# Attention's matmuls as 64x64 tiles, values in two PSUM banks, and VectorE adding the second bank in the drain

## The chip, the cores and the metric

The kernel runs on one core of one Trainium2 chip. Such a core has TensorE (PE in the profile, with its weight loads as PEld), VectorE (DVE), ScalarE (ACT), GpSimd (POOL) and SyncE (SP, which here only issues DMAs). TensorE reads SBUF and writes PSUM; VectorE and ScalarE read both; in this kernel GpSimd and the DMAs touch SBUF and DRAM alone. The metric is the device time of one execution in microseconds. Three timed executions of the kernel before took 3159.02, 3157.11 and 3157.24 us, so the median is 3157.24.

## The reference

The input x is 8 images of 512 channels and 32x32 places, in float32. Two blocks follow each other.

Layer 0 is an attention block of 8 heads with 64 channels each: group norm (32 groups), a 512 to 1536 projection, softmax attention over the 1024 places per head, a 512 to 512 projection, a second group norm, and the residual. Layer 1 is a single-head attention over all 512 channels with normalised weights and a root-mean-square norm of the projections.

```python
hn  = group_norm(x, gn1_scale, gn1_bias)
q, k, v = split(einsum('bchw,oc->bohw', hn, w_qkv) + b_qkv)      # per head: 64 channels x 1024 places
wgt = softmax(einsum('bct,bcs->bts', q * 64**-0.25, k * 64**-0.25))
a   = einsum('bts,bcs->bct', wgt, v)
x   = x + group_norm(einsum('bchw,oc->bohw', a, w_proj) + b_proj, gn2_scale, gn2_bias)
# layer 1
q, k, v = split(rms_normed(einsum('oc,bcn->bon', w_qkv1, x)))
x   = (x + w_out1 @ (softmax(q.T @ k * 512**-0.5) applied to v)) / sqrt(2)
```

## The kernel before

**Order.** Every engine is wrapped in `InOrder` (L24), so each engine executes its instructions in the order in which the code writes them. What stands earlier in an engine's queue and waits holds up all that stands behind it, SP's DMAs too. All arithmetic is float32; the hardware runs each float32 matmul as two passes, each with its own weight load, so the profile counts two matmul records for one in the code.

**Memory.** `Slots` (L39) hands out seven SBUF tiles of 16 KB per partition, first freed, first taken. PSUM has eight banks: `ps_s` holds three tiles of two banks (`wide` and the scores), `ps_m` two tiles of one bank (`bank`).

**Attention of layer 0**, the class `Heads` (L562). The eight heads are taken as four pairs j; a pair's two heads lie on partitions 0 to 63 and 64 to 127 (`halves`). For each pair the 1024 query places are eight rows of 128, so a batch has 32 steps i = 8j + r. One `step` (L635) does, in this order: `softmax(i)` (VectorE takes each head's maximum, ScalarE takes exp from PSUM and sums it); in every second step from i = 5 on, i odd, the `values` (L610) of a group of two earlier rows; the functions in `fill`, among them in even steps one piece of the projection that makes the next pair's q and k; `scores(i + 1)`; `turn`, in which VectorE transposes the probabilities of the step before and SP sends them in four DMAs to the group's tile pT; then `scale`, in which GpSimd divides the probabilities by their sum; last the functions in `later`, among them GpSimd's adds for the projections.

Scores are matmuls over the 64 channels of a head, on 64 rows and 128 columns of the array, the two heads in turn. Values are matmuls over 128 key places with 64 output channels, on 128 rows and 64 columns, the two heads in turn, all added in one bank `po`; ScalarE moves that to `a`, with the bias.

**Projections.** `project_rows` (L398) makes q and k in batch 0, and pair 0 of each next batch. It splits the 128 input channels in two halves of 64 rows with one bank each; ScalarE moves both out and GpSimd adds them. `project_seven` (L476) serves pairs 1 to 3 of the later batches: seven products stand for the eight of q and k over both halves of the places. Product 0 uses all 128 rows and one bank, the products 1 to 3 of both halves run as pairs on 64 rows each. Each of its four pieces (product 0; pairs 1, 2, 3) is one `yield`, and so one even step. As the first piece is short, the loop over i (L1433) puts two of the eight parts of the next values beside it in the first step of pairs 1 and 2 (`values(..., 2)`); the bank stays open till the step after.

**Drain.** After the 32 steps two groups of values are left, 14 and 15. Between them lie products of the next batch's v (`project_v7`, in the profile p_v_B and p_v_T), whose sums VectorE drains from three `ps_s` tiles. The code around it, with L1505 to L1525:

```python
heads.values(STEPS // RG - 2)      # group 14
heads.turn()                       # transpose of step 31, and its four DMAs
Seven.drain()                      # VectorE's waiting drains
fetch("proj7", b)                  # SP: weights of the output projection
...                                # VectorE: sums of a; ten products of v
heads.values(STEPS // RG - 1)      # group 15
...
finish_layer0(...)                 # output projection: p_o_B first, then p_o_T
```

The last batch has no next v; `LastOut` (L665) covers its drain with shares of its output projection (pp in the profile).

**Norm of batch 1 in batch 0's steps.** From i = 14 (k = 0 at L1461) the steps of the group norm's coefficients run one per step; two of them are a small matmul on TensorE (pm, pv) with a `ps_m` bank, and VectorE follows each.

## Time and profile before

| | |
|---|---|
| median of three timed executions | 3157.24 us |
| profiled execution | 3158.3 us |
| its span | 3156.5 us |
| granted TensorE clock, mean | 0.998 |
| PE busy | 3128.6 us, 13014 matmul records |
| s (scores), 64 rows x 128 columns, 512 wide | 2048 records, 510.5 us |
| po (values), 128 rows x 64 columns, 256 wide | 4096 records, 473.4 us |
| pq (project_seven), 64 x 128 | 1008 records, 452.8 us |
| pq, 128 x 128 | 84 records, 40.9 us |
| pqk (project_rows), 64 x 128 | 640 records, 144.3 us |
| DVE busy | 2366.4 us |
| ACT busy | 1070.1 us |
| POOL busy | 1409.5 us |

A busy time is the union of an engine's records within the group. Matmuls overlap each other, and their ends are modelled, so the distance from one start to the next tells more than the length of a record. In the timeline, a row merges neighbouring instructions of one kind: start, length, engine, line, operation, output and inputs with shapes (for PE, rows*columns of the tile used), their number, and in brackets the idle time of the engine before them with what ended it. All instructions bear L34, the line of the recording helper, so the names of tiles tell them apart.

### The profile page before, as it was taken

What the parts mean: (1) busy time and instruction counts of PE and PEld (TensorE: products, weight loads), DVE (VectorE), ACT (ScalarE), POOL (GpSimd) and SP (SyncE); (2) the same over time, 40 slices, a digit from 0 to 9 for tenths busy, and PEclk for the clock granted to TensorE, in tenths of its full rate; (3) what the DMA queues carried; (4) which work ended last, traced back from release to release, by engine and by line L of the source; (5) the groups of instructions that cost most, each with busy time, mean ns of one, the idle gap of its engine ahead of it and who ended that gap; (6) DMA issues with size and microseconds to landing.
All of it is one profiled execution on the core that took longest, in us unless ns stands there. A gap on an engine that the chain in (4) does not pass through costs nothing.

```text
span 3156.5 us, 36568 instructions
## 1 busy us (share of the span) xinstructions
PE 3128.6 (99%) x13014; PEld 1613.1 (51%) x13014; DVE 2366.4 (75%) x3213; ACT 1070.1 (34%) x1844; POOL 1409.5 (45%) x1129
## 2 busy tenths in 40 slices
PE   9999999999999999999999999999999999999899
PEld 5445544456444554545545555445554455444454
DVE  5697777876788767886678876787677877778765
ACT  2453124521245212551125502354133531245311
POOL 1554236732367314771247703566235642356124
PEclk9999999999999999999999999999999999999999
DMA  6777225862168521784128832388224872158600
GB/s 207 208 203 232 77 57 158 215 203 67 57 180 230 178 55 60 206 231 153 47 79 227 225 117 51 114 219 227 91 68 119 217 230 77 30 159 213 194 7 33
DMA packets 230317, 451.56 MB, mean 143 GB/s; under 512 B 22100, under 2 KB 62840, under 8 KB 224376
## 3 DMA queue, kind: packets, MB, share of 16 engines
q1 hardware_dynamic: 230016, 449.20, 50.4%
q8 instruction: 104, 1.70, 0.2%
q14 instruction: 77, 0.63, 0.1%
q10 hardware_dynamic: 120, 0.02, 0.0%
HBM read 137.26 MB, written 29.56 MB: 53 GB/s over the span
## 4 chain that ended last, share of the span: by engine, by line
PE 88%; DMA 3%; POOL 3%; DVE 3%; SPq 1%; issue 1%; ACT 0%; DVEq 0%; ACTq 0%; POOLq 0%
PE s L34 12%; PE po L34 12%; PE p L34 7%; PE p_v_T L34 6%; PE pq L34 6%; PE p_v_B L34 5%; PE py L34 4%; PE pqk L34 4%; PE pa L34 4%; PE p_u_T L34 4%; PE pe_e L34 3%; PE pe_bc L34 3%; PE pe_a L34 3%; PE p_o_T L34 3%; PE p_u_B L34 3%; DMA pT<-pb 2%
## 5 line engine op out<-in xcount | busy, mean ns | idle before, releaser
L34 ACT ACTIVATE p<-s,nm 128x1024 f32<-128x1024 f32 x512 | 565.6, 1109 | 796.0 <-DVE nm L34 461.0
L34 POOL TENSOR_SCALAR p<-p,tt 128x1024 f32<-128x1024 f32 x512 | 566.0, 1118 | 413.5 <-DVE tt L34 405.4
L34 DVE TENSOR_REDUCE nm<-s 128x1 f32<-128x1024 f32 x512 | 602.2, 1217 | 138.1 <-PE s L34 137.0
L34 DVE STREAM_TRANSPOSE pb<-p 128x2048 f32<-128x2048 f32 x256 | 590.0, 2305 | 54.7 <-DMA pT<-pb 36.2
L34 PE MATMUL s<-qk 64*128 64x512 f32 x2048 | 510.5, 605 | 0.7 <-POOL qk L34 0.5
L34 PE MATMUL po<-pT,v 128*64 128x256 f32 x4096 | 473.4, 383 | 2.4 <-DMA pT<-pb 1.5
L34 PEld LDWEIGHTS po<-pT,v 128*64 128x64 f32 x4096 | 283.2, 137 | 228.5 <-issue 29.9
L34 PEld LDWEIGHTS s<-qk 64*128 64x128 f32 x2048 | 193.2, 186 | 242.7 <-issue 214.5
L34 PE MATMUL p<-e,v 128*128 128x512 f32 (+1 forms) x520 | 229.9, 594 | 2.5 <-DVE x L34 2.5
L34 POOL TENSOR_TENSOR x<-x,o 128x1024 f32<-128x1024 f32 x21 | 52.1, 2509 | 349.0 <-ACT o L34 349.0
L34 POOL TENSOR_TENSOR esum<-esum,e 128x512 f32<-128x512 f32 x96 | 141.6, 1499 | 148.3 <-ACT e L34 148.3
L34 POOL TENSOR_TENSOR u<-u,xy 128x512 f32<-128x512 f32 x64 | 79.2, 1268 | 278.1 <-DMA xy<-far_rinv 273.5
L34 PE MATMUL pq<-hn,qk 64*128 64x512 f32 (+1 forms) x420 | 191.8, 593 | 0.0
L34 ACT ACTIVATE e<-e,shift,rinv 128x512 f32<-128x512 f32 x96 | 75.8, 810 | 269.0 <-DVE e L34 269.0
L34 DVE TENSOR_TENSOR v<-v,p_v_T 128x256 f32<-128x256 f32 x300 | 114.3, 416 | 68.8 <-PE p_v_T L34 50.0
L34 PEld LDWEIGHTS p<-e,v 128*128 128x128 f32 x520 | 98.1, 192 | 130.5 <-issue 121.3
L34 PE MATMUL pqk<-hn,qk 64*128 64x512 f32 (+1 forms) x672 | 158.2, 590 | 0.0
L34 PE MATMUL pq<-t,qk 64*128 64x512 f32 x336 | 151.0, 589 | 0.0
L34 PE MATMUL pq<-v,qk 64*128 64x512 f32 x336 | 150.9, 589 | 0.0
L34 POOL TENSOR_TENSOR esum<-e 128x512 f32<-128x512 f32 x16 | 25.1, 1586 | 274.7 <-ACT e L34 274.7
L34 PE MATMUL py<-x,gram 128*128 128x512 f32 x320 | 141.2, 601 | 4.4 <-DVE x L34 4.4
L34 POOL TENSOR_TENSOR qk<-qk,v 128x512 f32<-128x512 f32 x96 | 127.2, 1334 | 3.2 <-ACT v L34 1.6
(240 smaller groups left out, 4737.7 us busy)
## 6 DMA issues: line engine op xcount, KB each, us to landing
pT<-pb SPq DMA_DIRECT2D x1024, 256.0 KB, 4.6
qk<-far_qk SPq DMA_DIRECT2D x21, 896.0 KB
hn<-in_x_dram SPq DMA_DIRECT2D x32, 512.0 KB, 4.8
x<-in_x_dram SPq DMA_DIRECT2D x32, 512.0 KB, 3.9
out_dram<-x SPq DMA_DIRECT2D x63, 256.0 KB, 2.8
score<-far_score SPq DMA_DIRECT2D x8, 1792.0 KB, 11.8
value<-far_value SPq DMA_DIRECT2D x8, 1792.0 KB
proj<-far_proj SPq DMA_DIRECT2D x7, 1792.0 KB
```

Of the source, the lines that this page charges most:

```text
L34: return lambda *args, **kw: self._pin(call(*args, **kw))
```

## The change

A new helper `quads` issues each product as four matmuls of 64 rows and 64 columns: for each of two row halves, both column halves. Scores, both projections and values all use 64x64 tiles.

- `values` splits its 128 key places in two halves of 64 rows, each with a bank of its own. ScalarE moves the first bank to `a`, with the bias. The second bank is copied by ScalarE into the group's pT tile, which is no longer needed, and GpSimd adds that to `a`; in the drain's two calls VectorE adds the second bank from PSUM instead. pT is given back after that.
- `values` no longer runs in parts; the two parts beside the first piece of `project_seven` are gone.
- `project_seven` has again four pieces: product 1 with product 0 for the lower half of their columns, the same for the upper half, then products 2 and 3. Product 0 is split in two row halves, whose sums GpSimd adds.
- The small norm products of batch 1 are issued in even steps: the coefficient steps run two at k = 0 and k = 2, none at k = 1 and k = 3.

```diff
--- before.py
+++ after.py
@@ -370,6 +370,12 @@
     STEPS, LAG = CI * NB, 5
     halves = (slice(0, D), slice(D, P))
 
+    def quads(outs, left, right, first=True, last=True):
+
+        for out_, l, r in zip(outs, left, right):
+            for cs in halves:
+                PE.matmul(out_[cs], l[:, cs], r, start=first, stop=last)
+
     def project_qk(b, j, hn):
 
         qk = pair.tile([P, 2, N], F32, tag="qk", name=f"qk_{b}_{j}")
@@ -411,14 +417,7 @@
                     hs = slice(th * HN, (th + 1) * HN)
                     pms = [bank(f"pqk_{b}_{j}_{t}_{th}_{r}") for r in range(2)]
                     for ci in range(CI):
-                        for r in range(2):
-                            PE.matmul(
-                                pms[r],
-                                w[halves[r], ci, :],
-                                hn[halves[r], ci, hs],
-                                start=(ci == 0),
-                                stop=(ci == CI - 1),
-                            )
+                        quads(pms, [w[rs, ci, :] for rs in halves], [hn[rs, ci, hs] for rs in halves], ci == 0, ci == CI - 1)
                     to, rest = qk[:, 0, hs], spare[:, hs]
                     if t:
 
@@ -486,30 +485,41 @@
             return lambda: PO.tensor_add(to, a, b_)
 
         def pieces():
-            pm = bank(f"pq7_{b}_{j}_0")
-            run(matmuls(pm, [(w[:, k, :], right(None, 0, k)) for k in range(2)]))
-            AC.copy(tmp[1], pm)
-            yield [], []
             qk = pair.tile([P, 2, N], F32, tag="qk", name=f"qk_{b}_{j}")
             made(qk)
             kp = qk[:, 1, :].rearrange("p (be m) -> p be m", be=4)
             q1, q2 = (qk[:, 0, th * HN : (th + 1) * HN] for th in range(2))
             k1, k2 = (kp[:, :, th * P : (th + 1) * P] for th in range(2))
-            adds = (
-                ([], []),
-                ([], []),
-                ([add(q2, q2, q1), add(k2, k2, turned(q2))], [add(k1, k1, k2), add(k2, k2, turned(tmp[1]))]),
-                ([add(q1, q1, tmp[0]), add(q2, q2, tmp[1])], [add(q2, q2, tmp[2])]),
-            )
-            for n in range(1, 4):
+            adds = {
+                2: ([add(q2, q2, q1), add(k2, k2, turned(q2))], [add(k1, k1, k2), add(k2, k2, turned(tmp[1]))]),
+                3: ([add(q1, q1, tmp[0]), add(q2, q2, tmp[1])], [add(q2, q2, tmp[2])]),
+            }
+
+            def product(pms, n, cols, to):
+                count = CI if n else 2
+                for k in range(count):
+                    quads(
+                        [pm[:, to] for pm in pms],
+                        [w[rs, max(CI * n - 2, 0) + k, :] for rs in halves],
+                        [(right(r, n, k) if n else right(None, 0, k)[rs])[:, cols] for r, rs in enumerate(halves)],
+                        k == 0,
+                        k == count - 1,
+                    )
+
+            low, high = slice(0, TG), slice(TG, HN)
+            for n, cols in enumerate((low, high)):
                 pms = [bank(f"pq7_{b}_{j}_{n}_{r}") for r in range(2)]
-                for k in range(CI):
-                    for r in range(2):
-                        PE.matmul(pms[r], w[halves[r], CI * n - 2 + k, :], right(r, n, k), start=(k == 0), stop=(k == CI - 1))
-                if n == 1:
-                    AC.activation(q1, pms[0], AF.Identity, bias=bqs[:, j : j + 1])
-                    AC.copy(k1, turned(pms[1]))
-                elif n == 2:
+                product(pms, 1, cols, low)
+                product(pms, 0, cols, high)
+                AC.activation(q1[:, cols], pms[0][:, low], AF.Identity, bias=bqs[:, j : j + 1])
+                AC.copy(tmp[1][:, cols], pms[0][:, high])
+                AC.copy(k1[:, :, n * D : (n + 1) * D], turned(pms[1][:, low]))
+                AC.copy(q2[:, cols], pms[1][:, high])
+                yield [add(tmp[1][:, cols], tmp[1][:, cols], q2[:, cols])], []
+            for n in range(2, 4):
+                pms = [bank(f"pq7_{b}_{j}_{n}_{r}") for r in range(2)]
+                product(pms, n, slice(0, HN), slice(0, HN))
+                if n == 2:
 
                     AC.copy(q2, pms[0])
                     AC.activation(k2, turned(pms[1]), AF.Identity, bias=bkq[:, j : j + 1])
@@ -553,7 +563,7 @@
         def __init__(self, b, hn, v, qk):
             self.b, self.hn, self.v, self.a = b, hn, v, None
             self.qk = {0: qk}
-            self.pT, self.ps, self.waiting, self.open = {}, None, None, None
+            self.pT, self.ps, self.waiting = {}, None, None
 
         def scores(self, i):
             j, r = divmod(i, NB)
@@ -561,14 +571,11 @@
             self.ps = [ps_s.tile([P, N], F32, tag="sc", name=f"s0_{self.b}_{i}_{hh}") for hh in range(2)]
             for c in range(2):
                 cs = slice(c * HN, (c + 1) * HN)
-                for hh in range(2):
-                    PE.matmul(
-                        self.ps[hh][:, cs],
-                        qk[halves[hh], 0, r * P : (r + 1) * P],
-                        qk[halves[hh], 1, cs],
-                        start=True,
-                        stop=True,
-                    )
+                quads(
+                    [ps[:, cs] for ps in self.ps],
+                    [qk[rs, 0, r * P : (r + 1) * P] for rs in halves],
+                    [qk[rs, 1, cs] for rs in halves],
+                )
 
         def softmax(self, i):
             p = prob.tile([P, 4, 2, N // 4], F32, tag="p", name=f"p0_{self.b}_{i}")
@@ -607,28 +614,27 @@
                 PO.tensor_scalar(p[:, :, hh, :], p[:, :, hh, :], tot[:, hh : hh + 1], 1.0, ALU.mult, ALU.mult)
             self.waiting = (i, p)
 
-        def values(self, g, most=NT):
+        def values(self, g, engine=PO):
 
             j, t0 = g // (NB // RG), g % (NB // RG) * TG
-            po, s0 = self.open or (bank(f"po0_{self.b}_{g}", TG), 0)
-            s1 = min(s0 + most, NT)
-            self.open = (po, s1) if s1 < NT else None
+            pos = [bank(f"po0_{self.b}_{g}_{r}", TG) for r in range(2)]
             if self.a is None:
                 self.a = big(f"a_{self.b}")
-            for s in range(s0, s1):
-                for hh in range(2):
-                    ch = (2 * j + hh) * D
-                    PE.matmul(
-                        po[halves[hh], :],
-                        self.v[:, s, ch : ch + D],
-                        self.pT[g][:, :, :, hh, s, :],
-                        start=(s == 0),
-                        stop=(s == NT - 1),
-                    )
-            if self.open:
-                return
-
-            AC.activation(self.a[:, j, t0 : t0 + TG], po, AF.Identity, bias=col(BV, j))
+            pT = self.pT[g]
+            for s in range(NT):
+                for po, rs in zip(pos, halves):
+                    for hh in range(2):
+                        ch = (2 * j + hh) * D
+                        PE.matmul(
+                            po[halves[hh], :], self.v[rs, s, ch : ch + D], pT[rs, :, :, hh, s, :], start=(s == 0), stop=(s == NT - 1)
+                        )
+            a, rest = self.a[:, j, t0 : t0 + TG], pT[:, 0, 0, 0].rearrange("p B j -> p (B j)")
+            AC.activation(a, pos[0], AF.Identity, bias=col(BV, j))
+            if engine is VE:
+                VE.tensor_add(a, a, pos[1])
+            else:
+                AC.copy(rest, pos[1])
+                PO.tensor_add(a, a, rest)
             slots.give(f"pT_{self.b}_{g}")
             del self.pT[g]
 
@@ -1428,9 +1434,6 @@
             early, later = [], []
             if i < CI:
                 fill, later = fills[i] + fill, laters[i]
-            if b and r == 0 and 0 < j < CI - 1:
-
-                fill.append(lambda: heads.values((i + 1 - LAG) // RG, 2))
             if r == 0:
                 if j + 1 < CI:
                     if b:
@@ -1461,9 +1464,9 @@
                 k = i - 3 * CI - 2
                 if k == 0:
                     coeffs = norm1.gn.all_steps()
-                    early += [norm1.aggregate, lambda: next(coeffs)]
-                elif 0 < k < 8:
-                    early.append(lambda: next(coeffs, None))
+                    early.append(norm1.aggregate)
+                if 0 <= k < 8 and k not in (1, 3):
+                    early += [lambda: next(coeffs, None)] * (2 if k in (0, 2) else 1)
                 if 0 <= k - 7 < CI // 2:
                     for ci in range(2):
                         later.append(lambda ci=ci: norm1.apply(2 * (k - 7) + ci, PO))
@@ -1502,7 +1505,7 @@
             last = LastOut(b, heads, o_last)
             last.first_half()
             last.sums(0, 0)
-        heads.values(STEPS // RG - 2)
+        heads.values(STEPS // RG - 2, VE)
         heads.turn()
         if more:
             Seven.drain()
@@ -1522,7 +1525,7 @@
             for ci in (2, 3):
                 load_x(b, xt, ci)
             fetch("score", b)
-        heads.values(STEPS // RG - 1)
+        heads.values(STEPS // RG - 1, VE)
         slots.give(f"v0_{b}")
         if more:
             xt = big(f"x_{b}")
```

## Prediction

> **What bounds the kernel now.** First the page's parts 1 and 4: TensorE (PE) is busy 99% of the span and is 88% of the chain that ended last, so each microsecond in which PE streams nothing is a microsecond of the kernel.
>
> ```profile
> PE 3128.6 (99%) x13014; PEld 1613.1 (51%) x13014; DVE 2366.4 (75%) x3213; ACT 1070.1 (34%) x1844; POOL 1409.5 (45%) x1129
> PE 88%; DMA 3%; POOL 3%; DVE 3%; SPq 1%; issue 1%; ACT 0%; DVEq 0%; ACTq 0%; POOLq 0%
> ```
>
> Then the timeline of two attention steps of batch 3 (start, length, engine, operation).
>
> ```profile
> 1402.89 1.99 PE L34 MATMUL s<-qk 64*128 64x512 f32 x8
> 1404.71 3.60 PE L34 MATMUL pqk<-hn,qk 64*128 64x512 f32 x16
> 1404.91 2.36 DVE L34 TENSOR_REDUCE nm<-s 128x1 f32<-128x1024 f32 x2 [0.90 <-PE s L34]
> 1406.22 1.11 ACT L34 ACTIVATE p<-s,nm 128x1024 f32<-128x1024 f32 x1 [2.74 <-DVE nm L34]
> 1407.24 0.19 ACT L34 ACTIVATION_READ_ACCUMULATOR p<-s,nm 128x1 f32 x1
> 1407.33 1.10 ACT L34 ACTIVATE p<-s,nm 128x1024 f32<-128x1024 f32 x1
> 1408.14 1.88 PE L34 MATMUL s<-qk 64*128 64x512 f32 x8
> 1408.42 0.69 ACT L34 ACTIVATE qk<-pqk,bqs 128x512 f32<-128x512 f32 x1
> 1408.99 0.59 ACT L34 COPY spare<-pqk 128x512 f32<-128x512 f32 x1
> 1409.96 3.67 PE L34 MATMUL po<-pT,v 128*64 128x256 f32 x32
> ```
>
> Each fp32 product is two PE passes. 16 pqk records take 1408.14-1404.71 = 3.43 us: eight slots of 0.429, two tiles at once. A po slot (256 columns) is 0.2156 by the single records. The two steps are 2x4 slots of s, 8 of pqk and 16 of po: 10.31 us, but they repeat after 10.67 (1402.89, and the next s at 1413.56). The other 0.35 lies only where the tile shape changes: s to po 0.10 before it and 0.05 after its first slot, po to s 0.10 and 0.105. pqk to s, one shape, costs nothing.
>
> Last, the timeline of the drain after the 32 steps of that batch.
>
> ```profile
> 1427.69 2.31 DVE L34 STREAM_TRANSPOSE pb<-p 128x2048 f32<-128x2048 f32 x1 [2.34 <-POOL p L34]
> 1427.88 3.67 PE L34 MATMUL po<-pT,v 128*64 128x256 f32 x32
> 1431.60 0.47 ACT L34 ACTIVATE a<-po,cols 128x256 f32<-128x256 f32 x1 [6.78 <-PE po L34]
> 1432.37 0.75 DVE L34 TENSOR_TENSOR v<-v,p_v_T 128x256 f32<-128x256 f32 x2 [2.37 <-ACT v L34]
> 1433.13 1.26 SPq L34 DMA_DIRECT2D proj<-far_proj  x1
> 1436.05 2.73 DVE L34 TENSOR_TENSOR v<-v,p_v_T 128x256 f32<-128x256 f32 x8
> 1436.85 3.72 PE L34 MATMUL p_v_B<-v,hn 128*128 128x256 f32 x16
> 1440.50 3.67 PE L34 MATMUL po<-pT,v 128*64 128x256 f32 x32
> ```
>
> The last transpose runs beside the values of group 14; its four DMAs and then proj go out behind it on SP. By the packets, proj lands 11.3 to 14.0 us after the transpose's end (seven batches), and p_o_B, which needs it, starts at 1444.11 with 0 to 2.5 us to spare.
>
> **The change part by part.**
>
> *Tile shapes.* The program's order has 118 changes po to s (0.205) and 110 s to po (0.147); all go: -40.4 us. The 14 short pq7 products in 128x128 between s and po, with their own changes (0.10+0.10 and 0.09+0.05), go too: -4.8. Changes between attention and the 128x128 products of other stages stay, and I price them as now.
>
> *Streaming.* Twice as many matmuls of half the columns. If four tiles run at once, the slots are as many as before: s 439, po 442, pqk 137 us. pq7 pays 0.6 us for shorter slots. No row has 64x64; the nearest are 64x128 and 128x64, where two tiles start 7 ns apart and run beside each other, their weight loads too. Bounds: 0 (four together) to +1271 us (two at a time: all the attention slots, 1271, once more). I take 0, since tiles split both by rows and by columns run together here. For issue, values need 8 records per 0.2156 slot, 27 ns each. After a stall at 191.43 us PE's sequencer passed 64 such records in 1.39 us, 22 ns each. That is enough, by little.
>
> *Short pieces.* pq7's four pieces were 1.72, 3.43, 3.43, 3.43 us, with two of eight value steps moved beside the first; now 2.59, 2.59, 3.43, 3.43 and the values whole. Take 0 at the end of s, 1404.71. The first exp is read out at 1407.43, +2.72; only then is its PSUM tile free for the second head of the next s. A 2.59 us piece ends earlier: +0.19 us with 0.06 for the semaphore. Then the banks: ACT empties the piece after the second exp, from +3.71 (1408.42), now with four operations. Act 128x256 takes 0.47 (0.38 apart), copies 0.37 (0.27 apart by the two v copies of the drain): the last ends at +5.0. Values now need both banks; PE gets there at 2.78+1.72 = 4.50 and waits till 5.06: +0.56. Queued behind that wait: values, the next s, and by it DVE and ACT. For full pieces ACT ends at +4.87 and PE comes at 5.15: no wait, 0.2 to spare. This happens at i = 3, 8, 10, 16, 18 of seven batches (at i = 0 the fifth product covers it): 35x0.75 = +26.4. Bounds: 0, if ACT were early, to 35x1.3 if every copy took the 0.59 of a 512-column one. I take the 256-column rows.
>
> *Values in two banks.* ACT gets a copy (0.37) per group and POOL an add of 128x256 (half of 1.28, 0.64), ahead of the scaling in POOL's queue. In a value step ACT ends its pair at about +4.4 and the next piece wants the banks at +5.17. POOL's add ends at +5.1; scaling then ends at +7.35, and the transpose wants it at about +7.6. Nothing added, with 0.25 to spare; if that cover is gone the add costs up to 0.4 in each of 100 steps, 40 us. pT is given back after POOL's add, some 1.5 us later than now; it is refilled for use 20 us on. The same number of pT DMAs goes out, in the same order.
>
> *The drain.* VectorE's add for group 14 stands ahead of the last transpose in DVE's queue, and waits for po 14 and ACT. po's last slot starts at 1431.17; ACT ends at 1432.07, the add (0.42 by the v adds) lets the transpose start at 1432.5 and end at 1434.8 instead of 1430.0: 4.8 us later. Behind it: four pT DMAs and proj on SP, and on DVE the drains that free the banks of p_v. The latter: T2's drain frees T1's bank 0.5 late, T3's drain frees p_v_B's 1.9 later still, so the last values start 2.4 late. The former: proj lands 4.8 later; with each batch's own slack (1.1, 2.5, 0, 0.5, 0.3, 0, 0.3) p_o_B starts 3.7, 2.3, 4.8, 4.3, 4.5, 4.8, 4.5 later, 29 in all; I take 27, since the DMA before it is out of the way by then. The two run beside each other; the later counts. Bounds: 17 (DVE's alone) to 34. In the last batch the transpose ends at 2957.96 and the last po starts at 2965.79, having waited for pT. The add moves that end to 2964.5: +6.5, and the last add is bare: +0.5. Together +34. VectorE's add for group 15 is covered by p_o_B's 3.5 us.
>
> *Norm products.* Once, in batch 0: the same two small products at other steps; VectorE waits about 1 us for each inside a step with 0.5 slack. 0, bounds -1 to +2.
>
> *Sum.* -40.4 -4.8 +0.6 +26.4 +34 = +15.8 us against the profiled execution, 3158.3 us (span 3156.5 and 1.8 around it): 3174.1. The median of the runs shown is 1.1 lower, so 3173.
>
> A rule weighed against this: the Trainium skill, "TensorE: Matmul & The Clock Gate", Part 3, says that matmuls start and end strictly in program order. The program issues both passes of a tile before the next tile, so by that rule a second pass would hold up the other three tiles, four tiles would do the work of two, and the sum would be 3158+1271 = about 4430. In this trace the first passes of the two s tiles start at 1402.888 and 1402.895, the second tile ahead of the first's second pass: tiles overtake each other here, so I go by the row.
>
> **The rivals.**
> *A, faster: the short pieces don't wait.* If ACT empties the banks before PE comes, the 26.4 go and the time is 3147. For: ACT is busy only 34%. Against: its order puts the second exp first, and that ends at +3.81 in every ordinary step. It turns to faster when the wait is under 0.1 us in place of 0.75.
> *B: the second bank's copy or POOL's add is late in ordinary value steps too.* Margins are 0.2 to 0.3 us; 0.3 us in 100 steps gives 3203.
> *C: the four tiles don't all run at once*: up to 4430 (two at a time).
> *D: PE's issue binds in the values.* The densest lasting row is 54 ns per record; were that the limit, a group would take 6.9 instead of 3.45 us: +440, 3610. Against: the 22 ns above.
> *E: the drain is hidden*, because proj comes sooner without other traffic: 17 instead of 27, 3163.
>
> **How the numbers follow.** Main 53%, E 12%, A 13%, B 12%, C 5%, D 5%. The likeliest gives 3173 (its own range 3160 to 3188). C and D, 10%, stay out above; 3146 to 3215 holds the others but for some tails of A and B. A measurement tells 0.2% (6.3 us) from no change. Faster is most of A and a little of E: 0.15; within 0.2%, parts of E, A and main: 0.09; slower the rest: 0.76.
>
> **What the profile after would show.** Right: PE matmuls of 64*64 only, in s, po, pqk and pq; a pair of steps in batch 0 of 10.3 instead of 10.67 us; PE waiting for ACT before po after each short pq piece; in the drain the transpose only after po 14, and p_o_B after a wait for proj of a microsecond or more. Wrong: po groups longer than 3.5 us (C or D), no wait before po (A), p_o_B as early as now (E), or waits before pqk in every step (B).

## The result and the profile after

The changed kernel takes 3209.19 us (median of 4 runs, 3205.75 to 3213.86), the kernel before 3157.54 (4 runs beside it, 3157.11 to 3159.02): ratio 1.0165, 95% interval 1.0152 to 1.0177. It is slower, as forecast, but by 52 us where the sum said 16. It lies inside the stated range, which reached up beyond rival B's 3203; the sum's own range ended at 3188. The profiled execution took 3213.9 us (span 3212.1), 55.6 us more of span than the one before; the accounts below are between these two spans.

Parts 1 and 4 of the page of the kernel after, busy time by engine and the chain that ended last:

```profile
PE 3129.9 (97%) x22066; PEld 1717.4 (53%) x22066; DVE 2372.1 (74%) x3229; ACT 1112.4 (35%) x2061; POOL 1517.7 (47%) x1283
PE 61%; POOL 12%; issue 8%; DMA 8%; DVE 6%; SPq 3%; ACT 2%; DVEq 0%; POOLq 0%; ACTq 0%
```

PE is busy for as long as before (3128.6), with 9052 more instructions. What grew is the time in which it waits: PE's share of the chain fell from 88 to 61%, and GpSimd's (POOL) rose from 3 to 12% though it is busy less than half the time. What PE waited for, first after, then before (total us, times, longest):

```profile
PE s L34 <- POOL qk L34: 11.8, 18, 1.1
PE p_v_B L34 <- DVE v L34: 11.7, 7, 1.7
PE pq L34 <- DVE v L34: 6.2, 7, 0.9
PE p_o_B L34 <- DMA proj<-far_proj: 5.8, 4, 1.6
```

```profile
PE s L34 <- POOL qk L34: 0.5, 2, 0.4
PE p_o_B L34 <- DMA proj<-far_proj: 0.7, 2, 0.4
```

The two rows of p_v_B and p_o_B are the drain and were forecast. The two of s and pq were not: the scores of a new unit (one q and k, eight steps) wait for GpSimd's adds to q, and the first short piece waits for VectorE's v adds. The latter comes once in each of seven batches, the former 18 times, against twice before.

The drain of batch 3 (batches are counted from 0) in the timeline after:

```profile
1456.21 3.69 PE L34 MATMUL po<-pT,v 64*64 64x256 f32 x64 [1.69 <-issue]
1459.92 0.47 ACT L34 ACTIVATE a<-po,cols 128x256 f32<-128x256 f32 x1 [7.87 <-PE po L34]
1460.43 0.42 DVE L34 TENSOR_TENSOR a<-a,po 128x256 f32<-128x256 f32 x1 [7.83 <-ACT a L34]
1460.77 2.31 DVE L34 STREAM_TRANSPOSE pb<-p 128x2048 f32<-128x2048 f32 x1
1466.51 1.70 SPq L34 DMA_DIRECT2D proj<-far_proj  x1
1467.43 3.72 PE L34 MATMUL p_v_B<-v,hn 128*128 128x256 f32 x16 [1.68 <-DVE v L34]
1471.08 3.68 PE L34 MATMUL po<-pT,v 64*64 64x256 f32 x64
1476.26 1.10 PE L34 MATMUL p_o_B<-a,proj 128*128 128x512 f32 x2 [1.49 <-DMA proj<-far_proj]
```

The transpose that ran beside po 14 before now starts 4.56 us after po 14 does; behind it come proj's DMA and, on DVE, the drains that free PE's banks. A po group of 64 records of 64x64 takes 3.68 us, as the 32 of 128x64 did (3.67): four tiles run at once.

The first step of a batch (batch 3, i = 0) after:

```profile
1276.76 0.65 PE L34 MATMUL pq<-hn,qk 64*64 64x256 f32 x4
1276.95 0.69 DVE L34 TENSOR_TENSOR v<-v,p 128x512 f32<-128x512 f32 x1
1277.56 0.68 DVE L34 TENSOR_TENSOR v<-parts,p 128x512 f32<-128x512 f32 x1
1278.29 0.43 PE L34 MATMUL pq<-t,qk 64*64 64x256 f32 x2 [0.88 <-DVE v L34]
```

The piece needs two banks, one for each row half. The first row half (pq<-hn) has its bank and runs four records. The other (pq<-t) may not start until VectorE's two adds have emptied the second bank, in which the fifth of v's seven products lies. It starts 1.53 us after the first, of which PE stands idle for 0.88.

And the short piece of i = 8 with the values behind it, batch 4:

```profile
1717.31 2.14 PE L34 MATMUL s<-qk 64*64 64x512 f32 x16
1717.36 1.11 ACT L34 ACTIVATE p<-s,nm 128x1024 f32<-128x1024 f32 x1
1718.80 0.38 ACT L34 COPY v<-pq 128x256 f32<-128x256 f32 x1
1719.06 0.68 ACT L34 COPY qk<-pq 128x256 f32<-128x256 f32 x2
1719.24 0.19 PEld L34 LDWEIGHTS po<-pT,v 64*64 64x64 f32 x4 [0.67 <-ACT v L34]
1719.79 3.00 PEld L34 LDWEIGHTS po<-pT,v 64*64 64x64 f32 x58 [0.35 <-ACT qk L34]
```

The first row half of PE is through with its scores at 1717.31 + 1.72 = 1719.03, the second, which had waited for the first exp, 0.26 later. The last copy of the piece ends at 1719.74, and the second bank's tiles start there, 0.5 us late. The wait is where the prediction put it.

Where the steps changed: us against the kernel before, from the start of the last score matmul of step i to that of step i + 1, in the one profiled run of each kernel, as a mean over batches 1 to 7. The columns are the kernel after and six of the experiments below, in their order: the last transposes first; the four pieces of before; values in one bank; the load alone in the kernel before; VectorE adding in every value step, with the last transposes first; and VectorE adding at i = 5, 13, 21 and 29, with the last transposes first and the pieces of before. Row 31 is the drain, up to the next batch's first scores, as a mean over batches 0 to 6.

```
 i   after  turn_first  old_pieces  one_bank  before+load  VectorE all  VectorE i%8=5
 0    2.35     2.35       -0.04       2.35       0.00         2.35        -0.04
 3   -0.61    -0.61        0.03      -0.61       0.00        -0.61        -0.00
 4    0.55     0.55        0.00       0.55       0.00         0.55         0.00
 6    0.54     0.17        0.02       0.01       0.01         1.09         0.95
 7    0.58     0.69        0.89       0.09       0.49        -0.43        -0.46
 8   -0.30    -0.30       -0.30      -0.30      -0.00        -0.47        -0.48
 9    1.09     1.06        0.51       0.82       0.00         1.04         0.51
10   -0.91    -0.97       -0.12      -0.73      -0.12        -0.93        -0.12
11   -0.38    -0.27       -0.24      -0.18      -0.61         0.19        -0.20
12    0.01     0.01        0.01      -0.00       0.01         0.88         0.01
13   -0.35    -0.35       -0.35      -0.04       0.00        -0.35        -0.35
15    0.53     0.66        0.57      -0.04       0.23        -0.35        -0.30
16   -0.30    -0.30       -0.30      -0.30       0.15        -0.46        -0.35
17    1.06     1.06        0.51       0.82       0.00         0.71         0.51
18   -0.84    -0.84        0.00      -0.61       0.00        -0.83         0.00
19    0.24     0.03       -0.35      -0.04       0.00         0.03        -0.35
23    0.15    -0.13       -0.06      -0.04       0.26        -0.33        -0.26
31    4.79     1.30        4.84      -0.19       0.01        -0.21        -0.21
```

An undisturbed value step (13, 21, 25, 27, 29) gains 0.28 to 0.35, what the tile shapes promised. The drain loses 4.8, the first step 2.35, and the steps ahead of a new unit, 7, 15 and 23, lose where they should gain. The span's 55.6 us are: within the steps 12.1, the seven drains 33.5, the last batch's tail 9.6, the head 0.4.

### The profile page after: what moved, and what is told of

Same layout as the page of the kernel before. It is cut to its first block, busy times and chain, and to the rows that moved or that the text cites. A ratio compares the mean times of both kernels' runs of the same rounds, so it can differ in the third digit from the quotient of the medians.

```text
span 3212.1 us, 55636 instructions
## 1 busy us (share of the span) xinstructions
PE 3129.9 (97%) x22066; PEld 1717.4 (53%) x22066; DVE 2372.1 (74%) x3229; ACT 1112.4 (35%) x2061; POOL 1517.7 (47%) x1283
## 4 chain that ended last, share of the span: by engine, by line
PE 61%; POOL 12%; issue 8%; DMA 8%; DVE 6%; SPq 3%; ACT 2%; DVEq 0%; POOLq 0%; ACTq 0%
POOL p L34 6%; PE po L34 6%; PE s L34 5%; PE p_v_T L34 5%; DMA pT<-pb 5%; PE py L34 4%; PE p_v_B L34 4%; DVE pb L34 4%; PE p_u_T L34 3%; PE pe_a L34 3%; PE pe_e L34 3%; PE pe_bc L34 3%; PE p_o_T L34 3%; POOL qk L34 3%; PE pa L34 3%
## 5 line engine op out<-in xcount | busy, mean ns | idle before, releaser
L34 PE MATMUL s<-qk 64*64 64x512 f32 x4096 | 555.8, 593 | 13.8 <-POOL qk L34 11.8
L34 PE MATMUL po<-pT,v 64*64 64x256 f32 x8192 | 506.0, 379 | 6.0 <-DMA pT<-pb 3.1
L34 PEld LDWEIGHTS po<-pT,v 64*64 64x64 f32 x8192 | 361.6, 133 | 159.2 <-issue 22.0
L34 PEld LDWEIGHTS s<-qk 64*64 64x64 f32 x4096 | 206.3, 133 | 229.9 <-issue 152.2
L34 PE MATMUL pq<-hn,qk 64*64 64x256 f32 (+1 forms) x1680 | 202.3, 420 | 0.0
L34 PE MATMUL pqk<-hn,qk 64*64 64x512 f32 (+1 forms) x1312 | 162.9, 590 | 0.0
L34 PE MATMUL pq<-t,qk 64*64 64x256 f32 (+1 forms) x1008 | 156.2, 449 | 6.2 <-DVE v L34 6.2
L34 PE MATMUL pq<-v,qk 64*64 64x512 f32 x672 | 151.7, 590 | 0.0
L34 PEld LDWEIGHTS pq<-hn,qk 64*64 64x64 f32 x1680 | 100.0, 133 | 58.5 <-issue 30.3
```

Of the source, the lines that this page charges most:

```text
L34: return lambda *args, **kw: self._pin(call(*args, **kw))
```

## The experiments

**The last transposes ahead of the values of group 14.**

```
-        heads.values(STEPS // RG - 2, VE)
         heads.turn()
+        heads.values(STEPS // RG - 2, VE)
```

> The changed kernel with one move: in the drain the last transposes are issued ahead of the values of group 14, so that VectorE's add for group 14 no longer stands before them. Theory (the drain is the largest of the losses): in the trace after, the last slot of po 14 is followed by p_o_B after 16.68 to 18.24 us in seven batches, against 12.93 to 13.38 before, 29.0 us in all, and the last batch's tail is 9.6 longer. Both should go back but for the adds themselves: p_o_B 12.9 to 13.6 us after po 14, and a time of 3209 - 29 - 6 = about 3174 (3169 to 3180). Rival (the drain waits for proj or pT for another reason than the add, such as GpSimd's later queue or the give-back of pT): p_o_B stays 16 to 18 us after po 14 and the time stays within 8 us of 3209.

Measured: 3179.84 us, ratio to the kernel before 1.0066 (1.0049 to 1.0083). The drain of batch 4, from the timeline of this kernel:

```profile
1821.02 3.69 PE L34 MATMUL po<-pT,v 64*64 64x256 f32 x64
1821.31 2.31 DVE L34 STREAM_TRANSPOSE pb<-p 128x2048 f32<-128x2048 f32 x1 [2.67 <-POOL p L34]
1825.24 0.42 DVE L34 TENSOR_TENSOR a<-a,po 128x256 f32<-128x256 f32 x1 [1.62 <-ACT a L34]
1837.31 1.13 PE L34 MATMUL p_o_B<-a,proj 128*128 128x512 f32 x2
```

The transpose lies beside po 14 again and p_o_B waits for nothing. From po 14's last slot to p_o_B it is 12.99 to 13.17 us in six of seven batches (14.97 in the last), against 16.68 to 18.24. The order on DVE is what cost the drain: 29 of the 35 us expected came back. In the profiled run two drains stay long, those of batches 3 and 6, by 4.1 and 3.8 us; in batch 3 po 14 stopped for 1.4 us in its middle. Why those two, no run tells. The last batch's tail also keeps 5.0 of its 9.6 us. There VectorE's add for group 14 still stands ahead of its sums of pp, and PE waits 0.56 and 1.50 us for these before the last values.

**The four pieces of before.**

```
+            pm = bank(f"pq7_{b}_{j}_0")
+            run(matmuls(pm, [(w[:, k, :], right(None, 0, k)) for k in range(2)]))
+            AC.copy(tmp[1], pm)
+            yield [], []
-            for n, cols in enumerate((low, high)):
-                ...
-            for n in range(2, 4):
+            for n in range(1, 4):
                 pms = [bank(f"pq7_{b}_{j}_{n}_{r}") for r in range(2)]
                 product(pms, n, slice(0, HN), slice(0, HN))
```

> The changed kernel with the four pq7 pieces of before (product 0 alone, 128x128 in one bank, then three pairs of 512 columns), so that no piece has two short halves in two banks and GpSimd gets two adds fewer for each unit; the values stay whole, in two banks. Theory: the steps that lose at short pieces come back: i=0 (+2.35 us in seven batches, 16.5 in all), the 0.56 us waits for the banks at i=4, 9, 11, 17, 19 (about 20 us in all), against which the short products' own tile changes return (+4.8), and part of the late q adds of GpSimd at i=7, 15, 23 (16 in all): 3209 - 16 - 20 + 5 - 5 = about 3173 (3163 to 3190). Rival (the second bank's copy and add are what is late, whatever the piece): the steps behind a first piece still wait for ACT's copies, since PE comes to the values sooner behind a 1.72 us piece than behind a 2.59 us one; then the time is 3200 to 3215.

Measured: 3197.31 us, 1.0120 (1.0102 to 1.0139): 12 us of the 36 expected. The table says why. The loss of i=0 is gone, 2.39 us in each of seven batches, and the wait at 19. But i=3 and 4 add up to what they did (0.03, and -0.06 with the new pieces), and i=8 to 10 and 16 to 18 to a little more (0.09 and 0.21 for -0.12 and -0.08): behind a piece of 1.72 us PE comes sooner to the next scores and to the values, and waits there (in batch 4 at i=8 the weight loads of the second head's scores wait 0.57 us for ACT's exp, those of the values 0.43 us for ACT's copy). That part is the rival's. And i=7 and 15 lose as much as ever, with two GpSimd adds fewer for each unit.

**GpSimd's add of the second bank at the end of its step.**

```
-                PO.tensor_add(a, a, rest)
-            slots.give(f"pT_{self.b}_{g}")
+                def ended():
+                    PO.tensor_add(a, a, rest)
+                    slots.give(f"pT_{self.b}_{g}")
+                self.ending = ended
...
             for f in later:
                 f()
+            if self.ending:
+                self.ending()
```

> The changed kernel with GpSimd's add of the values' second bank (and the give-back of pT behind it) moved to the end of its step, behind the scaling and the adds of the pieces. Theory (GpSimd's queue, with this add in front, is what makes s wait for q at i=7, 15, 23, where it loses 16.2 us against the ordinary 0.35 gain): the waits of s for GpSimd's add of qk fall from 11.8 us to under 4 and the time to 3195 to 3201. Rival (these waits come from the longer chain of the pieces, whose own adds are last in the queue either way; or what GpSimd saves early is paid by a later add of the values): 3206 to 3212.

Measured: 3219.55 us, 1.0191 (1.0174 to 1.0207), 10 us slower than the kernel after: a miss. The waits of s for GpSimd rose to 13.8 us. Both expectations had taken the add to be in the way of its own step; the second half of the rival was nearest. The timeline of the kernel after shows what happens at the end of a unit (batch 4, i=13 to 15):

```profile
1738.66 2.14 PE L34 MATMUL s<-qk 64*64 64x512 f32 x16
1740.95 2.21 POOL L34 TENSOR_SCALAR p<-p,tt 128x1024 f32<-128x1024 f32 x2 [2.57 <-DVE tt L34]
1743.13 2.91 POOL L34 TENSOR_TENSOR qk<-qk 128x512 f32<-128x512 f32 x2
1746.00 0.72 POOL L34 TENSOR_TENSOR a<-a,pT 128x256 f32<-128x256 f32 x1
1746.71 2.21 POOL L34 TENSOR_SCALAR p<-p,tt 128x1024 f32<-128x1024 f32 x2
1748.88 1.28 POOL L34 TENSOR_TENSOR qk<-qk 128x512 f32<-128x512 f32 x1
1748.98 2.14 PE L34 MATMUL s<-qk 64*64 64x512 f32 x16
1750.24 1.55 POOL L34 TENSOR_TENSOR qk<-qk,v 128x512 f32<-128x512 f32 x1
1751.76 2.23 POOL L34 TENSOR_SCALAR p<-p,tt 128x1024 f32<-128x1024 f32 x2
1753.93 2.53 POOL L34 TENSOR_TENSOR qk<-qk,v 128x512 f32<-128x512 f32 x2
1755.29 1.95 PE L34 MATMUL s<-qk 64*64 64x512 f32 x16 [0.71 <-POOL qk L34]
1756.40 0.75 POOL L34 TENSOR_TENSOR a<-a,pT 128x256 f32<-128x256 f32 x1
```

From 1740.95 GpSimd runs with no gap worth naming; the first of the two adds at 1753.93 finishes q, and s starts at 1755.29 behind it. The add of i=13 (1746.00) stands inside that stretch, the one of i=15 (1756.40) behind it. The kernel before, in the same stretch:

```profile
1706.59 2.21 POOL L34 TENSOR_SCALAR p<-p,tt 128x1024 f32<-128x1024 f32 x2 [2.95 <-DVE tt L34]
1718.85 2.51 POOL L34 TENSOR_TENSOR qk<-qk,v 128x512 f32<-128x512 f32 x2
1720.45 1.99 PE L34 MATMUL s<-qk 64*128 64x512 f32 x8
```

GpSimd had no gap there either. From the scaling of i=13 to the q adds it took 12.26 us; in the kernel after it takes 12.98, and the 0.72 between them is the add. Moving each add back within its step leaves the first of them inside. Where the run lost time is another place: in the profiles the steps are 3.3 us shorter than in the kernel after, but the drains 5.0 and the last tail 3.9 longer. What lengthens these wasn't traced.

**Values as before, 128x64 in one bank.**

```
-            pos = [bank(f"po0_{self.b}_{g}_{r}", TG) for r in range(2)]
+            po = bank(f"po0_{self.b}_{g}", TG)
...
-                            po[halves[hh], :], self.v[rs, s, ch : ch + D], pT[rs, :, :, hh, s, :], start=(s == 0), stop=(s == NT - 1)
+                        po[halves[hh], :], self.v[:, s, ch : ch + D], self.pT[g][:, :, :, hh, s, :], start=(s == 0), stop=(s == NT - 1)
...
-                AC.copy(rest, pos[1])
-                PO.tensor_add(a, a, rest)
```

> The changed kernel with the values of before, 128x64 tiles in one bank: no second bank, no copy of it, no add on GpSimd or VectorE, none in the drain. All else stays, scores, pqk and pieces at 64x64. Theory (each part acts by itself): the tile shapes cost again 0.35 us for each round trip, +38 to +40; the drain gives back 29 + 9; GpSimd's queue loses one add a step, so that the late q adds go, -16 - 12*0.5 of the steps' other small delays; the second bank no longer has to wait for the short piece's copies, but the single bank of the values still waits for the first of the two, so of the 20 + 16 us at short pieces about half goes: 3209 + 39 - 38 - 20 - 18 = about 3172 (3160 to 3185). Rival (the second bank costs nothing beyond the drain; the losses at the pieces are those of the pieces alone): 3209 + 39 - 38 = 3210, and the steps i=0, 4, 9, 11 still lose.

Measured: 3171.06 us, 1.0044 (1.0029 to 1.0059), within the expected range. The drain is that of before (-0.19 in row 31), value steps gain 0.04 instead of 0.35, and 7, 15, 19 and 23 lose nothing to speak of. At 9 and 17 the step is 0.82 longer, which is the 0.86 of value matmuls that i=8 and 16 gave back, less 0.04: no wait is left there, against 0.55 in the kernel after. But i=0 (2.35) and i=4 (0.55) are unchanged: these two belong to the pieces, the others to the second bank.

**Both first moves together.** The last transposes first and the four pieces of before.

> The changed kernel with both moves: the last transposes ahead of the values of group 14, and the four pieces of before. Theory (the two losses lie in different places and add up): the first alone gave 3180 and the second 3197, from 3209, so together 3209 - 29 - 12 = about 3168 (3163 to 3174). Rival (they share a cause, the later start of each batch's transfers): 3174 to 3180.

Measured: 3163.37 us (10 runs), 1.0015 (1.0005 to 1.0024): the two add up, and 5 us more. In its profile the drains are 1.9 us longer than before and the last tail 0.7, where the first move alone left 9.1 and 5.0; why, no run tells.

**VectorE adds the second bank in every value step,** with the last transposes first, first with the new pieces, then with those of before.

```
-                AC.copy(rest, pos[1])
-                PO.tensor_add(a, a, rest)
+                self.ending = lambda: VE.tensor_add(a, a, pos[1])
...
             self.scale()
+            if self.ending:
+                self.ending()
```

> The changed kernel with the last transposes ahead of the values of group 14, and in every value step VectorE, not GpSimd, adds the second bank, straight from PSUM behind the step's transpose and reciprocal; ACT's copy of the bank goes too. Theory (GpSimd is full where a unit's q is finished: in the trace after it runs from 1740.95 to 1757.15 us with no gap, and the 0.72 us add in that row pushes the last q add, for which s waits): i=7 and i=15, which lose 0.69 and 0.66 us against the kernel before in the run with the first move alone, fall to 0.0 to 0.1, i=19 and 23 gain a little, seven batches: 3180 - 12 = about 3168 (3162 to 3173). Rival (VectorE, busy 4.8 of 5.15 us in a step, is late itself with 0.42 us more, so that the next maxima and with them all steps move): 3180 to 3200.

> All three: last transposes first, the four pieces of before, the second bank added by VectorE at the end of the step. Theory: the run with the first two (expected 3168) less the 10 to 12 us of GpSimd's adds: about 3157 (3150 to 3163), what the kernel before takes; left of the change's gain of 0.35 us a value step is then what the bank waits of 0.5 us at i=9 and 17 take back. Rival (VectorE becomes late): 3165 or more.

Measured: 3171.36 us, 1.0040 (1.0025 to 1.0055), and 3155.30 (10 runs), 0.9991 (0.9977 to 1.0005). At i=7, 15 and 23 the gain of the tile shapes is there at last (-0.43, -0.35, -0.33), so GpSimd's add was in its way. Part of it comes back: i=6 and 12 lose 1.09 and 0.88, where a piece follows at once and waits for the bank that VectorE now empties behind a late transpose. The wait of weight loads for it, in the first of the two kernels:

```profile
PEld pq L34 <- DVE a L34: 20.6, 26, 2.4
PEld pqk L34 <- DVE a L34: 13.6, 19, 2.3
```

**The load alone, in the kernel before.** ACT copies each value result once more, GpSimd adds the copy to itself; nothing reads it.

```
             AC.activation(self.a[:, j, t0 : t0 + TG], po, AF.Identity, bias=col(BV, j))
+            if g < STEPS // RG - 2:
+                rest = self.pT[g][:, 0, 0, 0].rearrange("p B j -> p (B j)")
+                AC.copy(rest, po)
+                PO.tensor_add(rest, rest, rest)
```

> The kernel before with the cost alone: in each value step ACT also copies the 128x256 result into the part of pT that is done with, and GpSimd adds that copy to itself (a value that nothing reads); everything else is as it was. Theory (GpSimd's queue is full there already before the change, and s of a new unit starts 0.3 us after its last q add): i=7 and 15 lose 0.7 us each in seven batches and i=23 a part of that: +10 to +14, about 3169. Rival (the added GpSimd work is covered, and the losses at i=7 and 15 come from the matmuls' new order): within 3 us of 3157.

Measured: 3161.33 us (10 runs), 1.0008 (0.9998 to 1.0017): not to be told from no change, a quarter of what was expected. The places are the expected ones, i=7 +0.49, 15 +0.23, 23 +0.26, and the waits of s for GpSimd rose from 0.5 to 6.6 us; i=11 gives 0.61 back. So the add alone does delay the scores of a new unit, but by less than in the kernel after. A likely reason, which no run isolates: in the kernel after PE comes 0.35 us sooner each value step, so the unit's end is set by GpSimd and no longer by PE. Then the add costs its 0.2 to 0.5 us, and the gain that stood there is lost as well.

**VectorE adds at some steps, GpSimd at the others.** Both with the last transposes first and the four pieces of before; VectorE (written None, as in the kernels above at the step's end) at i=7, 15, 23, 31, and then at i=5, 13, 21, 29.

```
-                self.values((i - LAG) // RG)
+                self.values((i - LAG) // RG, None if i % NB == NB - 1 else PO)
```

> The version with the last transposes first and the four pieces of before (3163), but VectorE adds the second bank behind the step's transpose and reciprocal at i=7, 15, 23 and 31, where the next scores need a new unit's q from GpSimd; at the other value steps GpSimd adds as it did. Theory (each adder is late in its own steps: GpSimd at i=7, 15 and 23, 0.95, 0.37 and 0.02 us behind the kernel before, and VectorE only where a piece follows at once, i=6 and 12, 1.1 and 0.9): the steps 7, 15 and 23 fall to -0.35 and the steps 6 and 12 stay as in the version with GpSimd alone: 3163 - 7 x (1.3 + 0.7 + 0.3) = about 3148 (3143 to 3153), faster than the kernel before by 0.2 to 0.4%. Rival (what is gained at i=7 comes back in the steps behind it, as it did with VectorE everywhere): 3154 to 3163.

Measured: 3160.85 us (11 runs), 1.0010 (1.0001 to 1.0019): a miss. i=15 still loses 0.62. Its timeline, batch 4, from i=13:

```profile
1709.12 0.73 POOL L34 TENSOR_TENSOR a<-a,pT 128x256 f32<-128x256 f32 x1
1709.83 2.22 POOL L34 TENSOR_SCALAR p<-p,tt 128x1024 f32<-128x1024 f32 x2
1717.07 2.51 POOL L34 TENSOR_TENSOR qk<-qk,v 128x512 f32<-128x512 f32 x2
1718.40 1.09 PE L34 MATMUL s<-qk 64*64 64x512 f32 x8 [0.62 <-POOL qk L34]
```

The add that was moved away is the one behind the q adds; the one inside the packed stretch (1709.12) stayed, and the stretch, from the scaling at 1704.08 to the q adds, is 12.99 us as in the kernel after.

```
-                self.values((i - LAG) // RG, None if i % NB == NB - 1 else PO)
+                self.values((i - LAG) // RG, None if i % NB == NB - 3 else PO)
```

> As the version before it, with the last transposes first and the four pieces of before, but VectorE takes over the second bank's add two steps earlier, at i=5, 13, 21 and 29, and GpSimd keeps i=7, 15, 23 and 31. Theory (what is late at i=15 is GpSimd's add of the step two before, i=13: it stands at the head of a stretch that runs without a gap up to the unit's last q add, while the add of i=15 itself stands behind that q add and can't matter; this is why moving the add of i=15 left 0.62 us there): i=15 falls to -0.35, i=23 too, i=7 to about -0.4 with 0.8 more at i=6: against 3162, 7 x (0.95 + 0.3 + 0.5) = 12 less, about 3150 (3146 to 3156). Rival (it is ACT's copies or the pieces that are late, not GpSimd's order): i=15 stays at 0.4 to 0.6 and the time at 3159 to 3164.

Measured: 3153.57 us (11 runs; the kernel before 3157.10 in 15), 0.9986 (0.9977 to 0.9995). The same stretch:

```profile
1705.37 0.40 DVE L34 TENSOR_TENSOR a<-a,po 128x256 f32<-128x256 f32 x1
1705.84 2.22 POOL L34 TENSOR_SCALAR p<-p,tt 128x1024 f32<-128x1024 f32 x2
1713.08 2.53 POOL L34 TENSOR_TENSOR qk<-qk,v 128x512 f32<-128x512 f32 x2
1714.42 1.95 PE L34 MATMUL s<-qk 64*64 64x512 f32 x16
1715.55 0.74 POOL L34 TENSOR_TENSOR a<-a,pT 128x256 f32<-128x256 f32 x1
```

Between the two kernels VectorE's adds have changed places with GpSimd's, here i=13 for i=15. The stretch (from 1700.78) is down to 12.30 us, and s starts with no wait of PE's; all waits of s for GpSimd fell from 13.1 to 0.4 us. i=15 goes from +0.62 to -0.30, i=7 from +0.96 to -0.46. Part comes back one step earlier, where VectorE now adds: i=6 loses 0.95 in place of 0.19, i=14 0.30 in place of 0.11. This version is faster than the kernel after and lies 0.14% below the one before, less than the 0.2% taken as telling for one comparison, though its interval leaves out no change.

## Why the prediction was right in sign and wrong in size

Between the profiled runs the sum came out 40 us too low, and that the range held the time is luck: rival B, which stretched it, did not come true as it was put. Two of its steps failed. *"Nothing added, with 0.25 to spare"*, of the values in two banks, was worth 16.2 us; *"at i = 0 the fifth product covers it"* was worth 10.7. The drains, the last batch's tail included, came 9.1 higher than priced, the short pieces 6.1 lower, and 9.6 lie in steps that the sum did not name. The drain, for which the change was forecast to be slower, is the largest loss, and it came for the reason given.

Summed as the prediction summed, profile against profile:

```
                                            predicted  measured
tile shapes and streaming, where they show      -44.6     -44.6 less what is lost below
short pieces, i = 3, 8, 10, 16, 18 and the
  steps behind them                             +26.4     +20.3
first step of a batch, i = 0                      0       +10.7
values in two banks, i = 7, 15, 23                0       +16.2
other steps of batches 1 to 7 (5, 6, 24 to 30)    0        +6.6
batch 0                                           0        +3.0
drains between batches                          +27       +33.5
last batch                                       +7        +9.6
```

with 0.4 for the head, the time ahead of the first scores: 55.7, against the 55.6 measured. The measured column is what the steps lie above their slots, over all batches: seven times 2.35 - 0.82 at i=0, and seven times 0.58 + 0.53 + 0.15 + 3 x 0.35 at 7, 15 and 23. "By slots" means by counting the matmuls that run side by side, 0.429 us for each set of 512 columns and 0.2156 for 256, and the changes of shape. (35 x 0.75, in the prediction, is 26.25.)

- *Tile shapes*: right. Single value steps gain 0.352 us, to the third digit, where nothing else ends the step.
- *Streaming*: right; rivals C and D fall. A po group takes 3.68 us, as before. The Trainium skill, "TensorE: Matmul & The Clock Gate", Part 3, has matmuls start and end strictly in program order; by that a po group of 64x64 would, as an estimate, have taken about twice the 3.68 us that it does, so the measurement decides against the page here, as the two s tiles' starts had.
- *Short pieces*: right in place and kind, rival A falls. By slots, i=3 should have shrunk by 0.84 (2.59 for 3.43) and shrank by 0.61: the wait of the next scores for the first exp is 0.23, where 0.19 was forecast. Step 4 is 0.55 longer, and steps 9 and 17 by 0.55 more than slots and shapes make them (0.86 - 0.35 = 0.51, measured 1.06): the bank wait is 0.55, where 0.56 was forecast. But i=10 and 18 shrank by 0.84 in most batches, all that the slots give: no wait for the exp there, and behind them 0.38 at 19 in most batches and next to none at 11. Steps 8 and 16 are -0.54 by slots (the longer piece, the values and the shape changes that left) and lie 0.24 above that. As means, 0.79 at 3 and 4, 0.75 at 8 to 10, 0.80 at 16 to 18, 0.57 at 11 and 19 make 2.9 a batch, 20.3 in seven, for 26.4.
- *"at i = 0 the fifth product covers it"*: wrong, this sentence failed. The fifth product is no cover but the hindrance: it holds the second bank until VectorE has added it out. By slots i=0 should be 0.82 longer (+0.87 for the piece, about -0.05 for its shape changes, since a 128x128 product of v stands beside it in both kernels); it is 2.35 longer, and with a first piece of one bank not at all. The 1.53 between are the time by which the second row half starts behind the first in the rows above (1276.76 and 1278.29).
- *"Nothing added, with 0.25 to spare"* of the values in two banks: wrong. The margin was worked out against the transpose, within one step. The reader behind GpSimd's queue that has no slack is another one, the next unit's scores, up to two steps on; over a unit's last steps GpSimd is full, and was so before the change. Rival B had the right engine and the wrong steps: its 0.3 us in 100 ordinary steps didn't happen, about 0.77 us in 21 steps did.
- *The drain*: right, rival E falls. po 14 to p_o_B grew by 29.0 us over seven batches for 27 predicted; the transposes ended 3.56 us after po 14 for 3.63; the last values came 2.25 later for 2.4. The other 4.5 of the 33.5 lie elsewhere between the batches, mostly in the first four, and weren't traced to a cause; nor was what the last tail took beyond its 7.
- *Norm products*: batch 0 is 1.7 us shorter where the tile shapes would give 4.7. Of the 3.0 lost, 1.5 lie at i=15 and 17, where these products run. The kernel with the values in one bank has the same norm products and loses nothing at these two steps, so the loss comes only with the second bank; how, wasn't traced.

What stays open: the 5 us of i=5 and 6 in the kernel after, which come in batches 1 to 3 of the profiled run and not in others (there the weight loads of the scores wait 0.9 to 1.6 us for ACT's exp, and what makes that late wasn't traced); the drains of batches 3 and 6 with the transposes first; the longer drains when GpSimd's add stood at the end of its step. Values at 64x64 in a single bank weren't tried: the Trainium skill, "PSUM — Partial Sum Buffer", "PSUM bank collisions raise a hardware error", says that two row tiles can't write one bank at the same time, which no run here shows.

## What to carry to other kernels

A queue that is half idle on average can be full for the three steps that matter: sum its work between the event that starts it and the one that PE waits for, and ask whether PE will soon come earlier. When a result is split in two banks, follow both banks to their last holder, and follow the add that joins them past its own reader, to all who stand behind it in that engine's queue. A join that stands ahead of what feeds a transfer is better put behind it: that gave back 29 us here.

## What the runs showed of the hardware

Two row halves with a bank each can run at different phases on PE. At i=9 of batch 4 the tiles of the free bank started at 1719.24 and ran four records, those of one key place; then they stood still too, until the other bank's tiles started at 1719.79, and the step lost 0.55 us. From there on the first row half stayed ahead: its next scores started at 1722.87, while values of the second half still started at 1723.08. Nor do starts keep the program's order across row halves: two values tiles of i=7 started at 1707.96, ahead of two score tiles at 1708.08 that the program issues before them. Four 64x64 tiles stream at the rate of two of 128x64 or 64x128, and issue keeps up with 8 records (four matmuls, four weight loads) per 0.2156 us slot: two steps with a pqk-sized piece take 10.32 us (scores at 1738.66 and 1748.98), the 10.31 that their slots need. VectorE's add of a 128x256 result from PSUM took 0.42 us, against 0.38 of ACT and 0.72 of GpSimd for the same sum by way of a copy.
